# Identity transposes in TensorE's planned pauses, and low-rank products in row groups of their own, in a twelve-stage decoder on one core

## The chip, the core and the metric

The kernel runs on one core of one Trainium2 chip. The metric is the device time of one execution in microseconds (us), as the median of several runs. The core's engines, each with its own instruction stream, are TensorE (PE, matrix products; its weight loads appear as PEld), VectorE (DVE), ScalarE (ACT), GpSimd (POOL) and SyncE (SP, which here issues most DMAs). TensorE's clock can be throttled; the profile reports the granted clock as a share of full speed.

## The reference

The reference is a pre-norm decoder of four layers on x of shape 4 x 256 x 128 in f32, with a context of 4 x 512 x 96. Every layer has self-attention, cross-attention and a feed-forward part, each added to the residual:

```python
x = x + _L0_attn_ref(_layernorm(x, axis=-1), L0_attn_W, L0_attn_b)
x = x + _L0_xattn_ref(_layernorm(x, axis=-1), ctx_768, ...)   # 16 heads of 64, low-rank terms, 4 image tokens
x = x + _L0_ffn_ref(_layernorm(x, axis=-1), ...)              # grouped attention and 8 experts
...
x = x + _L3_attn_ref(_layernorm(x, axis=-1), ...)
x = x + _L3_xattn_ref(_layernorm(x, axis=-1), ctx_768, ...)
x = x + _L3_ffn_ref(_layernorm(x, axis=-1), ...)              # itself 6 layers of local attention and gated feed-forward
```

What the change touches in the arithmetic's layout is the first cross-attention. There each of the four weights has a low-rank term of rank 32:

```python
def _lora(t, down, up, alpha):
    return t @ down @ up * (LORA_W * alpha[0] / RANK)
q_in = x @ Wq + _lora(x, q_down, q_up, q_alpha)
k_in = org_ctx @ Wk + _lora(org_ctx, k_down, k_up, k_alpha)
v_in = org_ctx @ Wv + _lora(org_ctx, v_down, v_up, v_alpha)
out = _attention(q_in, k_in, v_in) + _attention(q_in, ipa_ctx @ Wk_ipa, ipa_ctx @ Wv_ipa)
return out @ Wo + bo + _lora(out, o_down, o_up, o_alpha)
```

## The kernel before

All four batches stay in SBUF as x (two tiles of 128 tokens by 128 features each). The twelve stages are written out as small named operations, per batch and per pair of heads: attn0, X0, F0, A1, X1, ffn1, A2, xattn2, ffn2, attn3, X3 (class `Net`), then six layers of local attention (class `LocalBlock`, from about 1130 us on). The string `ORDER` (L2496) interleaves the stages' batches as they are written: "attn0 X0 attn0 X0 attn0 F0 ...", so batch 0 of the first attention comes ahead of the first cross-attention's weights.

No operation is issued where it is written. `Flow.op` (L188 on) records it with its engine, a cost in us and a lateness from the table `NET` (L2236) or `LOCAL`, its reads and writes, and the buffers that it needs. `Flow.order` (L208) then plays a list schedule: it keeps a time for each engine, takes the engine whose next operation can start first, and among the operations that can start then, the one with the smallest due time. The due time is the running sum of TensorE's costs up to the operation's unit, less the rest of its own chain, plus its lateness. A buffer of a kind with a few slots (the eight PSUM banks among them) is given out when its last users have ended in this play. `Flow.issue` (L309) emits the operations in the order found; on the chip every engine runs its own list strictly in that order and waits on semaphores for true dependences. So the plan's times fix only the order; the chip's times are its own. A pause of TensorE in the plan is the time between the end of its last operation there and the planned start of the next.

Ahead of the plan, `Decoder.prepare` (L85) makes the identity on GpSimd, issues the loads of x, of columns, rows and the context, and builds masks.

The change and the prediction's steps touch these places:

- `Net.mm` (L393) and `Net.transpose` (L396): every product and every transpose of `Net`; a transpose is one product with the 128 x 128 identity as the moving operand.
- `Net.fetch` (L403, DMA issue at L410): one weight load on SP's queue into one buffer.
- `one_head` (attn0): n_turn (two transposes), h_qk, h_v, h_scores, h_max (L534), h_exp (L541), h_turn (four transposes), h_pT (copy), h_weigh (four products), h_add (L565).
- `low_rank` (L803): for each of q, k, v and o a fetch of the 32 x 1024 factor (kind x4, four slots) and of the small factor (kind e2, five slots), a scaling of the small one by alpha / 32 on DVE (l_scale, L813), then for each half of 512 columns a product (l_mm, planned at 0.9 us on TensorE) into one bank and an addition to the weight on DVE (l_add, L833). All factors lie in partitions 0 to 31. The products of o are four small ones per half.
- `image_keys` (L836): two sets of eight products with the 16 image-token columns (i_kv), after which `cross_wide` (L616) begins: p_v, p_k, p_q, p_scores and so on.
- L1796: every product of the local block; L2012 and L2086 its transposes (turn, turn_p), L2002 and L2045 the GpSimd products ahead of them.

Of the kernel before, what the change touches and what calls it, by code (L numbers as in the profile page):

```python
# [26 lines left out]
ALU = mybir.AluOpType  # L27
# [3 lines left out]
P = 128  # L31
B, S, D = 4, 256, 128
NCTX, CD = 512, 96
# [5 lines left out]
RANK = 32  # L39
# [103 lines left out]
class Flow:  # L143
# [17 lines left out]
    REST = 2.5  # L161
    STALL = 1.0
    WAIT = 5.0

    def __init__(self, parts, slots, lags, tables, tiles, free, dense, port, after):
        self.kinds = {name: (*kind, *part[1:]) for part in parts for name, kind in part[0].items()}
# [41 lines left out]
    def order(self):  # L208
        bases = self.bases()
        left = dict.fromkeys(sorted(bases), 0)  # L210
        for op in reversed(self.ops):
            op["tail"] = op["w"] + max(
                [op["lag"] + o["tail"] for o in op["next"] if o["unit"] == op["unit"]], default=0.0
            )
            op["from"] = bases[op["unit"]] - op["tail"]
            op["due"] = op["from"] + op["late"]
            op["open"] = len({id(o) for o in op["needs"]})
            op["ready"] = 0.0
            left[op["unit"]] += 1
        free = dict.fromkeys(self.LAG, 0.0)  # L220
        self.made = made = dict.fromkeys(self.slots, 0)
        self.held = {k: [None] * n for k, n in self.slots.items()}
        table, shape, rest, port, done, oldest = None, "whole", -9.0, 0.0, [], 0
        units = list(left)
        waiting = {e: [op for op in self.ops if op["eng"] == e and not op["open"]] for e in free}

        def when(op):

            at, takes, new = op["ready"], [], {}
            for b in [b for b in {id(b): b for b in op["bufs"]}.values() if b.kind is not None and b.slot is None]:  # L230
                n = new[b.kind] = new.get(b.kind, -1) + 1
                if b.kind not in self.free and b.turn != n + made[b.kind]:
                    return None
                if n == 0:
                    new[b.kind, "free"] = self.vacant(b.kind)
                if n >= len(new[b.kind, "free"]):
                    return None
                since, slot = new[b.kind, "free"][n]
                at = max(at, since)
                takes.append((b, slot))  # L240
            return at, takes

        while len(done) < len(self.ops):
            best = None
            while not left[units[oldest]]:
                oldest += 1
            limit = bases[units[oldest]] + self.AHEAD
            for e, ops in waiting.items():
                times = [
                    (max(free[e], can[0], port * op["port"]), op, can[1])  # L250
                    for op in ops if op["from"] < limit and (can := when(op)) is not None
                ]
                if times:
                    first = min(t for t, *_ in times)
                    late = lambda o: o["due"] + (
                        (o["patience"] if o["tiles"][0] != shape else 0.0)
                        + (self.WAIT if o["dense"] and first < rest + self.REST else 0.0) if e == "PE" else 0.0
                    )
                    pick = min((c for c in times if c[0] <= first + 1e-6), key=lambda c: (late(c[1]), c[1]["i"]))
                    if best is None or first < best[0]:  # L260
                        best = first, *pick[1:]
            assert best, "no operation can start"
            at, op, takes = best
            e = op["eng"]
            op["at"] = at
            if op["table"] and op["table"] != table:
                at, table = at + self.TABLE, op["table"]
            if e == "PE":
                at += self.SWITCH * (op["tiles"][0] != shape) + self.STALL * (op["dense"] and at < rest + self.REST)
                shape = op["tiles"][1]  # L270
            op["end"] = free[e] = at + op["w"]
            if op["dense"]:
                rest = op["end"]
            if op["port"]:
                port = op["end"]
            waiting[e].remove(op)
            left[op["unit"]] -= 1
            for b, slot in takes:
                b.slot = slot
                made[b.kind] += 1  # L280
                self.held[b.kind][slot] = b
            for o in {id(o): o for o in op["next"]}.values():
                o["open"] -= 1
                o["ready"] = max(o["ready"], op["end"] + op["lag"])
                if not o["open"]:
                    waiting[o["eng"]].append(o)
            done.append(op)
        return done

    def vacant(self, kind):  # L290

# [17 lines left out]
    def issue(self):  # L309
        for op in self.order():  # L310
            for b in op["bufs"]:
                if b.kind is not None and b.t is None:
                    b.t = b.make(b.slot)
            op["fn"]()


# [14 lines left out]
class Net:  # L331
# [21 lines left out]
    def __init__(self, ctx, d):  # L353
# [4 lines left out]
        at, most = _layout(LocalBlock.LAYOUT, LocalBlock.TILES)  # L358
# [8 lines left out]
            {k: "e" for k in NET if k.endswith("_exp")} | {"exp": "e", "gelu": "g"}, NET_TILES | LOCAL_TILES,  # L367
            ("bank", *LocalBlock.TILES), ("scores", "weigh"), PORT, after,
        )
        self.n = 0  # L370
        self.x = [Buffer() for _ in range(B)]

# [30 lines left out]
    def fetch(self, kind, *parts):  # L403

        w = self.buf(kind)

        def dma():
            for name, lo, hi, rows, view in parts:
                out = w.t[:rows, lo:hi]
                self.nc.sync.dma_start(out=out if view is None else view(out), in_=self.a[name])  # L410

        self.op("fetch", dma, [], [w])
        return w
# [389 lines left out]
    def low_rank(self, w):  # L803

        nc, d = self.nc, self.d
        for m, rows in (("q", D), ("k", CD), ("v", CD), ("o", RANK)):
            low, high = ("down", "up") if m != "o" else ("up", "down")
            n = rows if m != "o" else D
            big = self.fetch("x4", (f"x0_{m}{high}", 0, 1024, RANK, None))
            small = self.fetch("e2", (f"x0_{m}{low}", 0, n, RANK, None))  # L810

            def scale(m=m, small=small, n=n):
                nc.vector.tensor_scalar(  # L813
                    small.t[:RANK, :n], small.t[:RANK, :n], d.col(f"x0_{m}al", rows=RANK), 1.0 / RANK,
                    ALU.mult, ALU.mult,
                )

            self.op("l_scale", scale, [small], [small])
            for h in range(2):
                ps = self.buf("bank")  # L820
                cut = slice(h * 512, (h + 1) * 512)

                def product(m=m, rows=rows, big=big, small=small, ps=ps, cut=cut, h=h):
                    if m != "o":
                        self.mm(ps.t[:rows, :], small.t[:RANK, :rows], big.t[:RANK, cut])
                        return
                    for i in range(4):
                        g = 4 * h + i
                        self.mm(ps.t[:, i * D : (i + 1) * D], big.t[:RANK, g * P : (g + 1) * P], small.t[:RANK, :D])

                r = rows if m != "o" else P
                self.op("l_mm", product, [big, small], [ps])
                self.op("l_add", lambda m=m, r=r, cut=cut, ps=ps: nc.vector.tensor_add(  # L833
                    w[m].t[:r, cut], w[m].t[:r, cut], ps.t[:r, :]), [ps, w[m]], [w[m]])

    def image_keys(self):  # L836

# [860 lines left out]
    def write(self):  # L1698
        stages = {name: getattr(self, f"stage_{name}")() for name in STEPS if name != "F3"}
        self.last = LocalBlock(self)  # L1700
# [4 lines left out]
        self.last.write()  # L1705

    def stage_attn0(self):
        w = self.fetch("ws", ("a0_w", 0, 384, P, None))
        for b in range(B):
            self.one_head(b, w, P, 1.0 / math.sqrt(128.0), True, False)  # L1710
            yield
# [519 lines left out]
def slots():  # L2231
# [9 lines left out]
    "n_scale": ("DVE", 0.55, -8.91),  # L2241
    "n_scale4": ("DVE", 1.18, 121.06),
    "n_turn": ("PE", 0.25, 0.35),
    "n_out": ("ACT", 0.34, 8.73),
    "add": ("DVE", 0.45, 11.52),
    "fetch": ("SP", 0.3, -134.71),
# [250 lines left out]
attn0 X0 attn0 X0 attn0 F0 X0 F0 attn0 F0 X0 A1 F0 F0 A1 X1 F0 F0 A1 X1 F0 ffn1 A1 X1 ffn1 A2 X1 A2  # L2497
ffn1 xattn2 A2 ffn1 xattn2 ffn2 A2 xattn2 attn3 ffn2 X3 xattn2 attn3 ffn2 X3 attn3 ffn2 X3 in attn3 in X3 in in
"""
STEPS = ("attn0", "X0", "F0", "A1", "X1", "ffn1", "A2", "xattn2", "ffn2", "attn3", "X3", "F3")  # L2500


# [171 lines left out]
```

## Time and profile before

| | |
|---|---|
| median of 3 runs | 2126.19 us (2120.12 to 2128.97) |
| the profiled execution, its own time | 2128.02 us |
| its span, first to last instruction | 2126.2 us |
| mean granted clock of TensorE | 0.977 |
| PE busy | 2036.1 us, 24181 instructions |
| PE weight loads busy | 1346.7 us |
| DVE, ACT, POOL busy | 1638.7, 1178.9, 990.8 us |
| transposes at L396 | 257.1 us, 1757 instructions |
| chain that ended last | PE 69%, DVE 21%, POOL 5%, issue 3%, ACT 2%, DMA 1% |

How to read it: the page first gives busy time by engine over the whole span, then the span in 40 slices of 53 us with the busy share in tenths, TensorE's granted clock in the row PEclk and DMA traffic. Groups of instructions follow by source line; a line such as L393 is a helper that all stages share, so groups are told apart by their shapes ("64*128 64x512" is a stationary operand of 64 rows by 128 columns and a moving one of 64 rows by 512 columns). The list of waits says for which instruction's result an engine stood still. In the timeline each row is a start, a duration, the engine, the operation and how many instructions were merged; in brackets stands the idle time before it and what ended it. Windows give, for a stretch, its length, each engine's busy time and instruction count, then the granted clock, the DMA share and GB/s. An f32 product appears as two records, a transpose as one.

### The profile page before, as it was taken

The numbers are of one execution on the slowest core, as the hardware profiler recorded it, in microseconds if no ns is written. First come the engines' busy times: TensorE is split into PE (matmuls) and PEld (weight loads), VectorE is DVE, ScalarE is ACT, GpSimd is POOL, SyncE is SP. The second block draws the span as 40 slices with busy tenths as digits, with TensorE's granted clock in tenths as the row PEclk, the third lists the DMA queues.
The fourth block names the chain that finished last, engine by engine and source line by source line (L and its number), as shares of the span: only waits on it lengthen the run. The fifth ranks groups of instructions, "written<-read, shape, count | busy, mean of one in ns | idle before, by whom it ended". The sixth has DMA issues, their size and how long they took to land.

```text
span 2126.2 us, 59285 instructions
## 1 busy us (share of the span) xinstructions
PE 2036.1 (96%) x24181; PEld 1346.7 (63%) x24181; DVE 1638.7 (77%) x4352; ACT 1178.9 (55%) x2668; POOL 990.8 (47%) x1155
## 2 busy tenths in 40 slices
PE   7999999999999999799999998999999999999997
PEld 4566585767665666566665656666656666666665
DVE  3766777788778678988887688789788787897882
ACT  1754736444545686476565564555556556556553
POOL 2333424331312234455365357557567465575660
PEclk6999999999999999899999999999999999999998
DMA  5000020011020000100000102112121121211101
GB/s 154 1 1 1 1 66 6 31 31 58 9 76 2 9 2 2 35 27 1 1 1 1 51 14 69 42 26 79 42 72 49 28 69 43 71 46 42 29 22 31
DMA packets 33422, 71.16 MB, mean 33 GB/s; under 512 B 5688, under 2 KB 17984, under 8 KB 33152
## 3 DMA queue, kind: packets, MB, share of 16 engines
q1 hardware_dynamic: 20320, 50.29, 8.0%
q10 hardware_dynamic: 12832, 17.09, 2.5%
q8 instruction: 191, 3.13, 0.6%
q14 instruction: 79, 0.65, 0.1%
HBM read 41.68 MB, written 0.52 MB: 20 GB/s over the span
## 4 chain that ended last, share of the span: by engine, by line
PE 69%; DVE 21%; POOL 5%; issue 3%; ACT 2%; DMA 1%; POOLq 0%; SPq 0%; ACTq 0%; DVEq 0%
PE bank L393 39%; PE bank L1796 18%; PE bank L396 9%; PE bank L2012 2%; DVE arena L1950 2%; DVE arena L1960 2%; POOL arena L2002 2%; DVE arena L1965 2%; POOL arena L1964 1%; DVE arena L1573 1%; POOL arena L2045 1%; PE bank L2086 1%; DVE arena L2053 1%; DVE arena L2055 1%; DVE arena L1985 1%
## 5 line engine op out<-in xcount | busy, mean ns | idle before, releaser
L393 PE MATMUL bank<-arena 128*64 128x256 f32 (+11 forms) x6824 | 875.6, 395 | 11.5 <-ACT arena L1495 3.6
L393 PEld LDWEIGHTS bank<-arena 128*128 128x128 f32 (+4 forms) x6824 | 540.1, 166 | 291.1 <-issue 108.1
L1796 PE MATMUL bank<-arena 64*64 64x32 f32 (+3 forms) x13584 | 653.9, 251 | 11.4 <-ACT arena L2109 4.8
L1796 PEld LDWEIGHTS bank<-arena 64*64 64x64 f32 (+2 forms) x13584 | 387.9, 127 | 217.9 <-issue 119.8
L401 ACT COPY arena<-bank 128x512 f32<-128x512 f32 (+4 forms) x586 | 270.0, 489 | 295.2 <-PE bank L393 209.2
L396 PE MATMUL bank<-ident,arena 128*128 128x128 f32 x1757 | 257.1, 282 | 36.1 <-DVE arena L440 16.9
L396 PEld LDWEIGHTS bank<-ident,arena 128*128 128x128 f32 x1757 | 199.0, 143 | 134.3 <-issue 46.0
L1964 POOL TENSOR_TENSOR arena<-arena 128x1024 f32<-128x1024 f32 x96 | 226.5, 2363 | 123.1 <-DVE arena L1950 63.0
L675 POOL TENSOR_SCALAR arena<-arena 128x508 f32<-128x508 f32 (+1 forms) x256 | 175.8, 693 | 209.2 <-DVE arena L672 183.9
L670 ACT ACTIVATE arena<-bank,arena 128x508 f32<-128x508 f32 (+1 forms) x256 | 175.3, 691 | 79.1 <-DVE arena L668 36.6
L2002 POOL TENSOR_TENSOR arena<-arena 128x1024 f32<-128x1024 f32 x96 | 180.8, 1903 | 71.9 <-DVE arena L1986 71.9
L1958 ACT ACTIVATE arena<-bank 128x512 f32<-128x512 f32 x192 | 114.0, 601 | 133.3 <-PE bank L1796 106.3
L668 DVE TENSOR_REDUCE arena<-bank 128x1 f32<-128x508 f32 (+1 forms) x256 | 164.3, 678 | 17.9 <-PE bank L393 17.7
L972 ACT ACTIVATE arena<-bank 128x512 f32<-128x512 f32 (+1 forms) x256 | 124.5, 582 | 64.1 <-PE bank L393 62.7
L401 DVE COPY arena<-bank 128x512 f32<-128x512 f32 (+1 forms) x196 | 125.9, 668 | 43.5 <-PE bank L396 29.6
L1960 DVE TENSOR_TENSOR arena<-bank,arena 128x512 f32<-128x512 f32 x192 | 127.7, 684 | 39.9 <-ACT arena L1958 38.7
L2045 POOL TENSOR_TENSOR arena<-arena 128x1024 f32<-128x1024 f32 x48 | 91.4, 1903 | 108.5 <-ACT arena L2018 62.7
L1950 DVE TENSOR_TENSOR arena<-bank,arena 128x256 f32<-128x256 f32 x384 | 138.8, 413 | 3.1 <-ACT arena L1958 2.7
L949 DVE TENSOR_REDUCE arena<-bank 128x1 f32<-128x512 f32 (+2 forms) x256 | 116.9, 515 | 21.4 <-PE bank L393 21.0
L2018 ACT COPY arena<-bank 128x512 f32<-128x512 f32 x192 | 103.1, 601 | 28.8 <-PE bank L2012 28.8
L1965 DVE TENSOR_REDUCE arena<-arena 128x16 f32<-128x1024 f32 x96 | 114.4, 1204 | 0.0
L430 POOL TENSOR_TENSOR arena<-arena,neghalf 128x2 f32<-128x2 f32 (+1 forms) x56 | 41.3, 742 | 156.4 <-DVE arena L429 139.2
(227 smaller groups left out, 2424.2 us busy)
## 6 DMA issues: line engine op xcount, KB each, us to landing
arena<-arena SPq DMA_DIRECT2D x48, 384.0 KB, 4.0
arena<-in_f_w SPq DMA_DIRECT2D x24, 512.0 KB, 3.5
arena<-in_f_wqkv ACTq DMA_DIRECT2D x18, 512.0 KB, 6.8
arena<-arena SPq DMA_DIRECT2D x48, 128.0 KB, 2.3
arena<-in_f_wo ACTq DMA_DIRECT2D x6, 512.0 KB, 3.6
arena<-in_f_w ACTq DMA_DIRECT2D x6, 341.0 KB, 3.9
arena<-in_f_w ACTq DMA_DIRECT2D x6, 192.0 KB, 6.6
arena<-in_x_wq SPq DMA_DIRECT2D x2, 512.0 KB
```

What stands on the lines that cost most here:

```text
L393: self.nc.tensor.matmul(out, lhsT, rhs, start=start, stop=stop)
L396: self.nc.tensor.transpose(out, in_, self.d.ident)
L401: return self.op(name, lambda: copy(out(), in_()), reads, writes, holds)
L668: self.op("p_max", lambda ps=ps, one=one: nc.vector.tensor_reduce(one(nmx), ps.t[:, :n], AX.X, ALU.max, negate=True), [ps], [most], [nmx])
L670: self.op("p_exp", lambda ps=ps, one=one, cols=cols: nc.scalar.activation(cols(), ps.t[:, :n], AF.Exp, bias=one(nmx), accum_out=one(sums)) ...
L675: nc.gpsimd.tensor_scalar(cols(), cols(), one(sums), 1.0, ALU.mult, ALU.mult)
L1796: self.nc.tensor.matmul(out, lhsT, rhs, start=start, stop=stop)
L1950: nc.vector.tensor_mul(heads(tmp.t[:, cut])[:, :, lo : lo + 32], heads(ps.t)[:, :, 32 - lo : 64 - lo], spread(1, lo, lo + 32),)
L1960: op("cosine", lambda cut=cut, ps=ps: nc.vector.tensor_mul(heads(out.t[:, cut]), heads(ps.t), spread(0, 0, 64)), [ps, w["tab"]], [out])
L1964: op("rotary", lambda: nc.gpsimd.tensor_add(out.t, out.t, tmp.t), [out, tmp], [out])
L1965: op("norms", lambda: nc.vector.tensor_reduce(ss.t[:, at : at + 16], heads(sq.t), AX.X, ALU.add), [sq], [ss])
L2002: nc.gpsimd.tensor_mul(heads(out.t), heads(out.t), rs.t[:, at : at + 16, None].to_broadcast([P, 16, 64]))
```

## The change

It has three parts.

1. `low_rank`: the factors of q, k, v and o are loaded into partitions 0-31, 32-63, 64-95 and 96-127. One l_mm operation per half of the columns issues the products of q, k and v one after the other, into three banks taken together; it reads the factors of all three. The six l_adds follow. The two operations of o come after these, reading partitions 96 to 127. In the plan the six l_mm of q, k and v become two, each at the same cost of 0.9 us.
2. A new operation warm, planned first: 34 transposes of the identity into a bank, written at the head of the first stage.
3. `Flow.order` notes, for each TensorE operation that takes new banks and starts more than 9 us into the plan after a planned pause of over 0.7 us, a number of fillers: 0.7 of the time for which TensorE and the bank are both free, divided by 0.11 us. `Flow.issue` emits that many transposes of the identity into the operation's own bank directly ahead of it. The played times do not contain the fillers.

```diff
+    IDLE = 0.7
+    FILL = 0.11
+    SETTLED = 9.0
...
             op["at"] = at
+
+            op["fill"] = [
+                (b, int(0.7 * (at - max(free[e], self.since(b.kind, slot))) / self.FILL))
+                for b, slot in takes if b.kind == "bank" and at - free[e] > self.IDLE
+            ] if e == "PE" and at > self.SETTLED else []
...
+    def since(self, kind, slot):
+        b = self.held[kind][slot]
+        return max((o["end"] + o["lag"] for o in b.users), default=0.0) if b is not None else 0.0
...
+            b, n = max(op["fill"], key=lambda f: f[1], default=(None, 0))
+            for _ in range(n):
+                self.keep(b)
             op["fn"]()
...
+        self.flow.keep = lambda b: self.transpose(b.t[:, :P], d.ident)
...
-                out = w.t[:rows, lo:hi]
+                out = w.t[rows if isinstance(rows, slice) else slice(rows), lo:hi]
...
     def low_rank(self, w):
...
-        for m, rows in (("q", D), ("k", CD), ("v", CD), ("o", RANK)):
+        parts = {}
+        for i, (m, rows) in enumerate((("q", D), ("k", CD), ("v", CD), ("o", RANK))):
+
+            r = slice(RANK * i, RANK * (i + 1))
...
+            big = self.fetch("x4", (f"x0_{m}{high}", 0, 1024, r, None))
+            small = self.fetch("e2", (f"x0_{m}{low}", 0, n, r, None))
...
+            parts[m] = big, small, r, rows
+        for h in range(2):
+            cut = slice(h * 512, (h + 1) * 512)
+            made = {m: self.buf("bank") for m in "qkv"}
+
+            def products(made=made, cut=cut):
+                for m, ps in made.items():
+                    big, small, r, rows = parts[m]
+                    self.mm(ps.t[:rows, :], small.t[r, :rows], big.t[r, cut])
+
+            self.op("l_mm", products, [b for m in "qkv" for b in parts[m][:2]], list(made.values()))
...
     def stage_attn0(self):
+        warm = self.buf("bank")
+        self.op("warm", lambda: [self.transpose(warm.t[:, :P], self.d.ident) for _ in range(WARM)], [], [warm])
...
+    "warm": ("PE", 0.1, -300.0),
...
+WARM = 34
```

More of the change, by code (lines that the diff above doesn't have):

```diff
@@ L805, in low_rank, with scale @@
         nc, d = self.nc, self.d
-        for m, rows in (("q", D), ("k", CD), ("v", CD), ("o", RANK)):
+        parts = {}
+        for i, (m, rows) in enumerate((("q", D), ("k", CD), ("v", CD), ("o", RANK))):
+            r = slice(RANK * i, RANK * (i + 1))
             low, high = ("down", "up") if m != "o" else ("up", "down")
             n = rows if m != "o" else D
-            big = self.fetch("x4", (f"x0_{m}{high}", 0, 1024, RANK, None))
-            small = self.fetch("e2", (f"x0_{m}{low}", 0, n, RANK, None))
-            def scale(m=m, small=small, n=n):
+            big = self.fetch("x4", (f"x0_{m}{high}", 0, 1024, r, None))
+            small = self.fetch("e2", (f"x0_{m}{low}", 0, n, r, None))
+            def scale(m=m, small=small, n=n, r=r):
@@ L813, in scale @@
                 nc.vector.tensor_scalar(
-                    small.t[:RANK, :n], small.t[:RANK, :n], d.col(f"x0_{m}al", rows=RANK), 1.0 / RANK,
-                    ALU.mult, ALU.mult,
+                    small.t[r, :n], small.t[r, :n], d.col(f"x0_{m}al")[r], 1.0 / RANK, ALU.mult, ALU.mult,
                 )
             self.op("l_scale", scale, [small], [small])
[L819 to L834, printed above, removed]
@@ new lines, in low_rank @@
+            parts[m] = big, small, r, rows
[7 more added lines that the diff above has]
+            self.op("l_mm", products, [b for m in "qkv" for b in parts[m][:2]], list(made.values()))
+            for m, ps in made.items():
+                n = parts[m][3]
+                self.op("l_add", lambda m=m, n=n, cut=cut, ps=ps: nc.vector.tensor_add(
+                    w[m].t[:n, cut], w[m].t[:n, cut], ps.t[:n, :]), [ps, w[m]], [w[m]])
@@ new lines, in low_rank, with product @@
+        big, small, r, _ = parts["o"]
+        for h in range(2):
+            ps = self.buf("bank")
+            cut = slice(h * 512, (h + 1) * 512)
+            def product(ps=ps, h=h):
+                for i in range(4):
+                    g = 4 * h + i
+                    self.mm(ps.t[:, i * D : (i + 1) * D], big.t[r, g * P : (g + 1) * P], small.t[r, :D])
+            self.op("l_mm", product, [big, small], [ps])
+            self.op("l_add", lambda cut=cut, ps=ps: nc.vector.tensor_add(
+                w["o"].t[:, cut], w["o"].t[:, cut], ps.t), [ps, w["o"]], [w["o"]])
```

## The prediction

> **What bounds the kernel now.** I read the page's head first, then TensorE's waits, then its order of time at the start, then granted clocks in 1 us slices.
>
> ```profile
> span 2126.2 us, 59285 instructions
> ...
> PE   7999999999999999799999998999999999999997
> ...
> DVE  3766777788778678988887688789788787897882
> ...
> PEclk6999999999999999899999999999999999999998
> ```
>
> TensorE (PE) is busy in nearly every slice, VectorE (DVE) in about eight tenths. PEclk is below 9 in the first slice (53 us), around 800 us and at the end. A PE-bound kernel gains from less PE work, from a higher PE clock and from shorter pauses. So: where are the pauses?
>
> ```profile
> PE bank L396 <- DVE arena L440: 16.9, 6, 10.0
> PE bank L2012 <- POOL arena L2002: 12.8, 15, 1.4
> PE bank L2086 <- POOL arena L2045: 9.4, 7, 3.2
> PE bank L396 <- POOL arena L1578: 5.7, 2, 4.5
> ```
>
> Columns: total us, times, longest. 10.0 is the wait for the first layernorm. Going through PE's timeline I count 44 pauses of 0.7 us or more, 71.7 us together: 10.0 at the start, 3.6 in the rest of the first 53 us, 0.7 between 53 and 800 (one pause), 14.2 from 800 to 1000, 11.1 from 1000 to 1300, 32.1 (29 pauses) after. From 53 to 780 PE is busy for 722.4 of 727 us (99.4%), its parts added up.
>
> The start in order of time (start, us, what), PE alone:
>
> ```profile
> 11.65 4.45 PE L393 MATMUL bank<-arena 128*128 128x256 f32 x12 [0.46 <-ACT arena L401]
> 17.47 0.90 PE L396 MATMUL bank<-ident,arena 128*128 128x128 f32 x4 [1.38 <-ACT arena L541]
> 20.60 12.61 PE L393 MATMUL bank<-arena 32*128 32x512 f32 x20 [2.23 <-DVE arena L813]
> 33.00 1.90 PE L393 MATMUL bank<-ctxT,arena 96*128 96x508 f32 x2
> 34.83 3.78 PE L393 MATMUL bank<-arena 32*128 32x128 f32 x16
> 40.40 6.85 PE L393 MATMUL bank<-ctxT,arena 96*128 96x16 f32 x32
> 57.82 1.04 PE L396 MATMUL bank<-ident,arena 128*128 128x128 f32 x8
> ```
>
> An f32 product shows as two records. The x20 group is the six low-rank products of q, k, v (12 records) and the first h_weigh (8, from 31.1): 10.5 us for six products, 1.75 each. A transpose costs 0.225 us here (0.90/4) and 0.13 later (1.04/8). The gap is the clock:
>
> ```profile
> 21.00:22.00 1.00, 1.00 (x2) 0.37 (x2) 0.00 (x0) 0.00 (x0) 0.00 (x0) 0.50 0.00 0
> ...
> 52.00:53.00 1.00, 1.00 (x5) 0.56 (x6) 0.00 (x0) 0.59 (x1) 0.00 (x0) 0.59 0.00 0
> 53.00:54.00 1.00, 1.00 (x8) 0.28 (x4) 0.47 (x3) 0.00 (x0) 0.00 (x0) 1.00 0.00 0
> ```
>
> The third number from the end is the granted clock: 0.50 until 52.8 us though PE has been busy without a hole since 20.6. Before 18.7 the rows print 1.00, but the x12 group (1,152 columns in two records each, 4.45 us; at 54.28 us eight records of 512 columns take 3.70, by which these would need 2.1) and the 0.225 us transposes show half speed already. Twelve us of products on 32 rows did not raise the clock; it rose after 5.7 us of products on 96 and 128 rows.
>
> **Part 1, the low-rank products.** The six products of q, k, v now lie in rows 0-31, 32-63, 64-95 and run as two groups of three. That three such products overlap, no row shows; the nearest has two 64-row products of 512 columns:
>
> ```profile
> 807.05 1.02 PE L393 MATMUL bank<-arena 64*128 64x512 f32 x4
> ```
>
> Two products took 1.02 us, where one alone needs 0.85 (1.75 halved, less latency). So a group of three costs between 1.75 us (full overlap) and 5.25 (none) at half clock; I take 1.85, the near row's overlap. Two groups: 3.7 instead of 10.5, so 6.8 us less. Each waits for what was queued for it:
>
> ```profile
> 12.90 7.34 DMA arena<-in_x_qdown
> 20.24 0.03 issue
> 20.27 0.29 DVE arena L813
> ```
>
> The first product waited for the small factor's DMA (landed 20.24) and one scale. Now it waits for the factors of k and v also; those were issued up to 0.9 us later, yet three scales ran back to back in 0.63 us from 20.27, so all had landed: 0.4 us later, with h_weigh and p_k queued behind on PE. The eight fetches stay eight of the same size on SP's queue; o's pair no longer stands behind products. The six l_adds (0.685 us each) can no longer hide between products: from 22.9 they run to 27.0, k's last to 26.4, when h_weigh ends too (24.7 plus 1.7). p_k then starts near 26.6, not 33.0: 6.4 us less, all on the path, since PE has one pause from there to 800. Eight banks exist and three are taken at once; no other product asks for them then.
>
> **Part 2, the clock of the start.** Warm-up: 34 transposes by 0.225 us are 7.7 us, from about 1.6 (identity made) to 9.3; the first true transpose starts at 10.01. They cost nothing; if each took 0.27 us (median of the rows), they would end at 10.8, and PE still idles 1.4 and 2.2 us before 20.6. They do not carry to 20.6 by themselves: PE then has nothing between about 16.6 and 21. What counts is after 21: two groups on 96 rows, h_weigh on 128, p_k on 96, some 7 us without a thin product, as long as what raised the clock at 52.8. So the clock is up near 27, not 52.8. Of 19.6 us of PE work from 33.0 to 52.6, 8.3 are long products (halved: 4.2) and 11.3 are loads of weights and transposes (0.21-0.225 to 0.13-0.14: about 3.8). Together 8 us; bounds 0 and 10, I take 7, as thin products may lower the clock for a while.
>
> **Part 3, fillers in the planned pauses.** The number is not in the trace: for each pause that the planner expects over 0.7 us, 0.7 of it divided by 0.11. If the plan's pauses are those of the trace after the first (43, 61.7 us), 393 transposes, 51 us at 0.13: inside the pauses, 0.83 of each. Cost: from 0 (each inside a true pause) to 51 and more (none is). I take 3.5, 27 fillers outside, because the planner's costs are near the rows (rotary 2.38, row 2.36; p_turn 0.47, row 0.52), so its pauses should be. A filler writes the bank of the operation behind it, so it waits for nothing that this operation didn't.
>
> Gain: after longer pauses the clock is 0.50 again: nine stretches from 811 to 2114 hold 48 us of PE work. By part 2's ratio (8 of 19.6) 20 us at most; half of it lies where DVE is as busy as PE (0.9 and more around 855-880 and 1299-1307), so 10 on the path; the fillers reach most: 8.
>
> A rule speaks against this. The Trainium skill, "TensorE: Matmul & The Clock Gate", Part 4, says that full clock does not engage for transposes, which don't count as busy. The rows:
>
> ```profile
> 1684.48 1.97 PE L2012 MATMUL bank<-ident,arena 128*128 128x128 f32 x8 [1.40 <-POOL arena L2002]
> 1686.24 3.96 PE L1796 MATMUL bank<-arena 128*128 128x512 f32 x12
> ```
>
> The clock is 0.50 from 1684.4 and 1.00 from 1687.2: 1.8 us of transposes and 1.0 of products raised it. Elsewhere (853.6 to 861.6) 1.5 us of products and more than twice as much transposing did. So I let transposes count; by the rule the 8 us fall away. The same page's window of 3.4 idle us before the clock falls is not what 1684.4 shows: 1.4 us sufficed after small products.
>
> **Sum.** 6.4 + 7 + 8 - 3.5 = 18 us less. The profiled execution took 2128.0 (span 2126.2 and 1.8 around it), so 2110; that is 1.8 above the median of the runs, so on the median 2108.
>
> **Rivals.**
> Fillers where there is no pause (0.22): one mechanism, PE's strict order. The plan has pauses that the chip fills, above all in 53 to 800, where the trace has one; there each filler costs its 0.13 us. Break-even: 18/0.13, some 140 more fillers outside pauses. If the plan pauses twice as long as the trace, 785 fillers, 102 us against 61.7: 40 lost, 21 gained: 2145. For it: PE is at 99.4% from 53 to 780. Against: the costs fit the rows.
> The gate ignores transposes (0.20), as the skill has it: 6.4 + 7 - 3.5, 10 less: 2116. Against: 1684 and 858.
> The planner moves (0.12): l_mm is charged 3.6 us instead of 7.2, so every later due time shifts alike, but its play of events shifts unevenly and picks another order, which the tuned due times do not fit. I give it 0.5% of loss, eating most: 2124. The trace can't tell.
>
> **How the numbers follow.** Forecast 0.46: 2108, own range 2095 to 2115. Below 0.5% (2115.6 to 2136.8 is no change that a measurement here can tell) I put nearly all of the forecast and a part of the second and third rival: faster 0.52; same 0.25; slower 0.23, nearly the first rival. The range reaches from the forecast's low end to most of the first rival: 2095 to 2140.
>
> **What would show it.** Right: two groups of three products near 21, p_k near 26.6, clock 1.00 by 28, PE's first true transpose still near 10, few slices under 1.00 after 800, pauses filled. Wrong: identity transposes between 53 and 800 with the stages there longer; clock still 0.50 after 30, or falling in filled pauses; the same work in another order with new waits.

## The result, and the profile after

| | before | after |
|---|---|---|
| median | 2127.3 us (14 runs, 2119.8 to 2134.1) | 2117.7 us (14 runs, 2111.1 to 2120.4) |
| ratio | | 0.9956 (95% interval 0.9943 to 0.9969): 9.4 us less |
| profiled execution: span, mean granted clock | 2126.2 us, 0.977 | 2118.5 us, 0.986 |

The direction was forecast, the size was not: about half of the 18 us came. The head of the page of after:

```profile
span 2118.5 us, 59911 instructions
...
PE   8999999999999998899999999999999999999998
...
PEclk8999999999999999999999999999999999999999
```

The clock's dip in the first slice is smaller, and those near 800 us and at the end no longer show in slices of 53 us (804 to 808 is still at half clock). 317 more TensorE records ran: the program holds 318 identity transposes, 34 for the warm-up, 45 before 27 us and 239 later. With these left out, TensorE's 24,181 records come in the same order in both profiles but for 18 of the first 92 (one record is missing from the trace of after): behind the start the planner did not pick another order. TensorE's waits (total us, times, longest), for the four rows shown of before:

```profile
PE bank L2044 <- POOL arena L2034: 12.2, 15, 1.4
PE bank L2118 <- POOL arena L2077: 9.2, 7, 2.1
PE bank L412 <- DVE arena L456: 8.5, 4, 4.4
```

The first two are almost unchanged (12.8 and 9.4 before): between 1290 and 2077 us, where the local block's transposes wait, the plan put no filler. In the third the wait of 10.0 us for the first layernorm is now 2.5, the rest being warm-up; the 4.4 near 1120 us is still open. The fourth (5.7 us before, for L1578) is no longer among the long ones.

The start of after, TensorE alone:

```profile
1.59 5.92 PE L412 MATMUL bank<-ident 128*128 128x128 f32 x34 [1.59 <-POOL ident masks.py:199]
...
15.49 2.69 PE L412 MATMUL bank<-ident 128*128 128x128 f32 x21
18.02 0.60 PE L412 MATMUL bank<-ident,arena 128*128 128x128 f32 x4
20.03 3.65 PE L409 MATMUL bank<-arena 32*128 32x512 f32 x20 [1.42 <-DVE arena L832]
23.51 2.78 PE L412 MATMUL bank<-ident 128*128 128x128 f32 x24
27.15 2.05 PE L409 MATMUL bank<-arena 32*128 32x128 f32 x16 [0.85 <-DVE arena L832]
29.12 8.48 PE L409 MATMUL bank<-ctxT,arena 96*128 96x16 f32 x34
```

The same 20 records that took 12.61 us take 3.65. But the next is not p_k, as I had it: it is o's low-rank products (32*128 32x128), ahead of which 24 fillers stand and TensorE still waits 0.85 us for L832, the scaling of o's factor. Then the image products (96x16, 32 of the 34 records) and the product behind them run 8.48 us, from 29.6 on at half clock:

```profile
28.00:29.00 1.00, 1.00 (x11) 1.00 (x9) 1.00 (x4) 0.00 (x0) 0.64 (x2) 1.00 1.02 414
29.00:30.00 1.00, 1.00 (x8) 0.88 (x8) 1.00 (x3) 0.00 (x0) 0.19 (x1) 0.81 0.90 356
30.00:31.00 1.00, 1.00 (x6) 1.00 (x6) 0.72 (x2) 0.00 (x0) 0.00 (x0) 0.50 0.68 188
```

TensorE is busy in all three rows (1.00 after the length), and the clock (third from the end) falls from 1.00 to 0.50, to come back at 39.9 us.

DVE's 4,352 instructions come in the same order in both programs, but for 22 places before 48 us. So each can be matched with itself, and the difference of its starts tells where time was won or lost. In the two profiles the lead is 10.4 us at 58 us, level to 540, 7.8 at 784, 10.7 at 890, 6.8 at 1136, 5.5 at 2104 and 7.6 at the end. I call this the lead below. It is read from one execution each: after, start_only, no_mid and seen (below) are one program up to 440 us, and their leads at 58 us are 10.4, 9.5, 8.7 and 8.9.

### The profile page after: what moved, and what is told of

The parts are those of the page before. It is cut to its first block, busy times and chain, and to the rows that moved or that the text cites. A ratio compares the mean times of both kernels' runs of the same rounds, so it can differ in the third digit from the quotient of the medians.

```text
span 2118.5 us, 59911 instructions
## 1 busy us (share of the span) xinstructions
PE 2050.2 (97%) x24498; PEld 1373.6 (65%) x24499; DVE 1638.8 (77%) x4352; ACT 1179.3 (56%) x2668; POOL 993.1 (47%) x1155
## 4 chain that ended last, share of the span: by engine, by line
PE 68%; DVE 22%; POOL 5%; issue 3%; ACT 2%; DMA 1%; POOLq 0%; SPq 0%; ACTq 0%; DVEq 0%
PE bank L409 39%; PE bank L1828 17%; PE bank L412 9%; PE bank L2044 2%; DVE arena L1982 2%; DVE arena L1992 2%; DVE arena L1997 2%; POOL arena L2034 2%; DVE arena L1603 1%; POOL arena L1996 1%; POOL arena L2077 1%; PE bank L2118 1%; DVE arena L2085 1%; DVE arena L417 1%; DVE arena L2087 1%
## 5 line engine op out<-in xcount | busy, mean ns | idle before, releaser
L409 PE MATMUL bank<-arena 128*64 128x256 f32 (+11 forms) x6824 | 857.5, 393 | 10.5 <-ACT arena L1525 3.6
L409 PEld LDWEIGHTS bank<-arena 128*128 128x128 f32 (+4 forms) x6824 | 532.6, 165 | 276.8 <-issue 100.0
L412 PEld LDWEIGHTS bank<-ident,arena 128*128 128x128 f32 x1757 | 196.6, 141 | 116.2 <-issue 47.3
L2044 PEld LDWEIGHTS bank<-ident,arena 128*128 128x128 f32 x768 | 87.0, 142 | 42.0 <-POOL arena L2034 21.8
```

The lines of the kernel that those rows point to most:

```text
L409: self.nc.tensor.matmul(out, lhsT, rhs, start=start, stop=stop)
L412: self.nc.tensor.transpose(out, in_, self.d.ident)
```

## The experiments

Ratios are to the kernel before, timed on the same chip, with 95% intervals; us are worked out on 2127.3.

**No filler after the start (start_only).**

```diff
-            ] if e == "PE" and at > self.SETTLED else []
+            ] if e == "PE" and 100.0 > at > self.SETTLED else []
```

> The changed kernel without its 239 fillers after the first 30 us (the 34 of the warm-up and the two groups of 21 and 24 stay). Theory A (the gain is made in the first 53 us, the later fillers cost what they bring): 10 us under before, ratio 0.9945 to 0.9955, and the same within 3 us as the changed kernel; in the profile the lead of 10.4 us at the first p_scores stays level from 440 to 784 us. Theory B (the later fillers bring the 8 us forecast less 3.5, and chance in the clock's windows hid it): 4 to 5 us slower than the changed kernel, ratio about 0.998.

Ratio 0.9972 (0.9962 to 0.9983), 6.0 us less. Lead 9.5 at 58 us, and level from 440 to 784 (9.5 at both). The profile is as theory A has it; the time lies between the theories: the later fillers together bring something like 3 us (about 0 to 7, so not clear of noise).

**No filler, warm-up and row groups kept (no_fill), and row groups alone (rows_only).**

```diff
-    SETTLED = 9.0
+    SETTLED = 1e9
...
-WARM = 34
+WARM = 0
```

The second hunk is in rows_only alone.

> The changed kernel with warm-up and row groups, but no filler at all. Theory A says the row groups are worth 6.4 us and the clock between 20 and 53 us the other 4: without fillers at 15 and 23 us TensorE is at half clock from 20, the two groups of products take 3.7 us instead of 1.8, and the clock rises near 27 to 30: 6 to 9 us under before (ratio 0.996 to 0.997). Rival (the fillers at 15 and 23 are idle work, the row groups do it all): 10 us under before, as the changed kernel.

> The row groups alone: no warm-up, no filler. The warm-up ends at 7.5 us and nothing carries its clock to 20: both theories expect the same as with the warm-up and without fillers, within 1 us, 6 to 9 us under before. If the warm-up's quicker first head (h_scores ends earlier) reached the path, this one would be slower by up to 2 us.

Ratios 1.0000 (0.9992 to 1.0008) and 0.9994 (0.9983 to 1.0004): no gain that the measurement can tell, where I had expected 6 to 9 us. The lead at 58 us is 3.9 and 4.4. A miss, and the profile of rows_only shows why. DVE and TensorE in order of time:

```profile
27.63 0.61 DVE L581 SCALAR_TENSOR_TENSOR x<-bank,arena,x 128x128 f32<-128x128 f32 x2 [2.43 <-issue]
28.16 0.68 DVE L850 TENSOR_TENSOR arena<-arena,bank 128x512 f32<-128x512 f32 x1
28.75 0.29 DVE L440 BATCH_NORM_STATS2 arena<-x 128x6 f32<-128x128 f32 x1
...
30.67 0.29 DVE L832 TENSOR_SCALAR arena<-arena,cols 32x128 f32<-32x128 f32 x1
30.99 0.68 DVE L850 TENSOR_TENSOR arena<-arena,bank 96x512 f32<-96x512 f32 x1
31.05 1.19 PE L409 MATMUL bank<-arena 32*128 32x128 f32 x4 [3.52 <-issue]
```

The scaling of o's factor (L832) stands on DVE's list behind h_add (L581, which waits for h_weigh), an l_add and the next batches' statistics (L440 on). Its data had been fetched some ten us earlier. TensorE, whose list has o's products next, stands for 3.52 us. In the kernel before that wait lay behind other products. The low-rank products and h_weigh before it, in no_fill:

```profile
21.70 6.33 PE L409 MATMUL bank<-arena 32*128 32x512 f32 x20 [3.56 <-DVE arena L832]
```

**Warm-up and fillers, products as before (no_rows).** The kernel after with the low_rank of before; the plan then has no group of 24 fillers near 23 us.

> Warm-up and all fillers, but the low-rank products as before, one after the other on 32 rows. Theory A: the row groups' 6.4 us are lost, the clock part stays only if 32-row products keep the clock up, which the profile of before speaks against: 0 to 3 us under before, ratio 0.9985 to 1.0005. Rival (the warm clock is what matters, the six products then take 5.3 us instead of 10.5): 5 to 8 us under before, ratio 0.9965 to 0.9975.

Ratio 0.9992 (0.9982 to 1.0003), 1.7 us less; as theory A. TensorE at the products:

```profile
21.14 11.57 PE L409 MATMUL bank<-arena 32*128 32x512 f32 x20 [2.56 <-DVE arena L829]
```

The clock is at 0.50 from 22.2 to 53.0 us, after fillers as without them. In no_mid and seen, with row groups, it fell near 22 us too, after waits of 2.4 and 2.2 us, but was back at 29. So in the time of the whole kernel neither part alone shows a gain; at 58 us this version leads by 0.2 us and the row groups without fillers by about 4, against 8.7 to 10.4 for both together. The reading is that the fillers need products on more rows behind them, and the row groups need something for the new wait.

**The image products made wider (wide_kv).**

```diff
-                        ps.t[:, 4 * B * g : 4 * B * (g + 1)], wi.t[:CD, g * P : (g + 1) * P],
-                        d.ctxT[:, :, NCTX - IPA :],
+                        ps.t[:, 16 * B * g : 16 * B * (g + 1)], wi.t[:CD, g * P : (g + 1) * P],
+                        d.ctxT[:, :, NCTX - 16 :],
...
```

> The changed kernel, with the 16 image-token products on 64 columns (the last 16 of each batch) instead of 16, the wanted columns picked in the copy after them; output as before. Theory A (the clock falls at 29 us because thin products count for little, though TensorE is busy): the clock stays 1.00 from 29 to 39, the products take about 5 us instead of 8.2, 3 to 5 us less than the changed kernel, ratio to before about 0.994. Rival (it falls because of a window in which TensorE waited for o's factor): clock 0.50 again from 29 to 39, no gain or a loss of up to 1 us.

Ratio 0.9957 (0.9939 to 0.9974), as after. The clock fell all the same, from 31 to 41 us, and the same 34 records took 7.4 us instead of 8.48. Theory A falls: 64 moving columns are no better than 16. The rival isn't shown either; see the open points.

**o's scaling moved up, the fillers ahead of o's products left out (scale_moved).**

```diff
-        for op in self.order():
+        done, groups = self.order(), 0
+        o_scale = [op for op in done if op["name"] == "l_scale"][3]
+        done.remove(o_scale)
+        done.insert(next(i for i, op in enumerate(done) if op["name"] == "h_add"), o_scale)
+        for op in done:
...
+            groups += n > 0
+            if n > 0 and groups == 2:
+                n = 0
```

> The changed kernel with the scaling of o's small factor moved ahead of h_add on DVE, and without the 24 fillers that stand ahead of o's products. Theory A (a new wait took the place of the one removed: o's products now follow at once and stand behind DVE's statistics of the next batch): o's products start near 23.6 instead of 27.2 us, 3 us less than the changed kernel, ratio about 0.994. Rival (something else, the image weights' DMA, is just as late): the image products start at 26 or later and under 1.5 us is gained.

Ratio 0.9960 (0.9945 to 0.9975): no gain. The wait is gone (o's products follow h_weigh without a gap), but in its profile the factors' DMA let the first group start at 21.6 instead of 20.0, after 3.0 us without work, and the clock was 0.50 from 22 to 42. That start is set by the landing of q's small factor and lies between 19.7 and 22.9 us in the 14 profiles, so one profile can't tell why the median didn't gain. That the wait and the clock have to be mended together was the guess that best (below) tests.

**Row groups alone, with the scaling moved (rows_scale).** The two edits of rows_only, and the first five added lines above.

> The row groups alone (no warm-up, no filler) with the scaling of o's small factor moved ahead of h_add. Theory A (the forecast's 6.4 us were there, and DVE's order took 3.5 of them back): the lead at 58 us is 7 to 8 us instead of 4.4, ratio to before 0.9965 to 0.998. Rival (the image weights' DMA is next and as late): the lead stays at 4 to 5 us, ratio 0.999.

Ratio 0.9975 (0.9964 to 0.9986), 5.3 us less; lead 7.6 at 58 us. As theory A: without a filler and without warm-up, moving one DVE instruction turned 1.3 us into 5.3 (a difference of about 1 to 7). Behind h_weigh TensorE goes on at 27.4 us, in rows_only at 31.05.

```profile
21.19 10.02 PE L413 MATMUL bank<-arena 32*128 32x512 f32 x36 [2.61 <-DVE arena L836]
```

The 36 records are both groups, h_weigh and o's products in one piece.

**No filler between 440 and 790 us (no_mid).**

```diff
...
+            groups += n > 0
+            if n > 0 and 3 <= groups <= 15:
+                n = 0
```

> The changed kernel without the 94 fillers between 440 and 790 us (13 places). Theory A (there the plan pauses and the chip does not): the lead of 10.4 us stays level to 784 instead of falling to 7.8, 2 to 3 us less than the changed kernel, ratio about 0.9945. Rival (the fillers lie in pauses too short to see, and the fall by 2.6 has another cause): no difference, 0.9956.

Ratio 0.9934 (0.9917 to 0.9952), 4.7 us less than after by the ratios (interval of the difference about 0 to 9). Against after, it gains 2.6 us between 540 and 763 us in the profile, as expected. Two of the rows taken out, as they are in after:

```profile
615.71 1.69 PE L412 MATMUL bank<-ident 128*128 128x128 f32 x14
...
634.75 1.16 PE L412 MATMUL bank<-ident 128*128 128x128 f32 x9
```

94 such transposes, some 12 us at 0.13, stand where before had no pause of 0.7 us or more. Against start_only, no_mid differs by the 145 fillers after 800 us: 0.9972 to 0.9934, 8 us gained (about 4 to 12).

**Twice the fillers (double).** FILL 0.055 instead of 0.11.

> The changed kernel with twice the fillers everywhere (614 instead of 318, the 34 of the warm-up unchanged), in the same places. Theory A prices a filler outside a pause at 0.13 us: 296 more are 38 us, of which the pauses that are still open there (about 10 us from 800 to 900 and at the end) hide a part: 20 to 30 us slower than the changed kernel, ratio to before 1.005 to 1.010. Rival (the fillers are hidden, since TensorE has slack that the profile counts as busy): under 10 us slower.

Ratio 1.0016 (1.0002 to 1.0030), 12.8 us over after for 296 more: 0.04 us for each, a third of what a transpose takes, at a mean clock of 0.992 in the profile. That lies between the theories: less than I had priced, more than the rival's 10. Between 548 and 763 us the lag on after grows by 7.2 us for some 90 more, 0.08 each; elsewhere they may lie in pauses or pay in clock, which was not taken apart.

**Fillers where the profile has the pauses (seen), and with the start mended (best).** seen is no_mid with this table, looked up by an operation's name and its number among those of that name; best adds ("l_mm", 0): 12, moves o's scaling, and drops the 24 fillers ahead of o's products.

```diff
+SEEN = {("turn", k): 9 for k in (32, 64, 96, 128, 160)} | {("turn", k): 5 for k in (72, 104, 136)}
+SEEN |= {("turn_p", 0): 12, ("turn_p", 6): 9, ("turn_p", 22): 7, ("turn_p", 38): 7, ("turn_p", 54): 7, ("turn_p", 70): 9}
+SEEN |= {("n_turn", 45): 28, ("n_turn", 51): 7, ("c_turn", 48): 7}
...
+            k = op["name"], kinds.get(op["name"], 0)
+            kinds[op["name"]] = k[1] + 1
+            if k in SEEN:
+                b, n = b or next(b for b in op["bufs"] if b.kind == "bank"), n + SEEN[k]
```

> The changed kernel without the 94 fillers between 440 and 790 us, and with 153 more, put by hand ahead of the 17 operations that paused 0.9 us or more for a result (not for a bank) in its profile: seven to nine ahead of the local block's transposes, 28 ahead of the layernorm transpose near 1120, 12 near 1292. Theory A (what pays is a filler in a pause that the chip has; nothing is lost there): no cold stretch at 1118, 1292, 1678, 1818, 1958, and 4 to 8 us under the kernel with the 94 left out, ratio to before 0.990 to 0.992. Rival (pauses and cold windows change place from run to run, so that fillers put where one profile shows a pause don't find it): same as that kernel, 0.9934.

> The one before, with the scaling of o's small factor moved ahead of h_add, the 24 fillers ahead of o's products left out, and 12 more ahead of the first low-rank products. Theory A (the clock then stays up from 15 us over the wait for the factors' DMA, and o's products follow at once): p_scores first at 38 to 39 us instead of 42, 3 us under the kernel before, ratio 0.988 to 0.991. Rival (the clock falls all the same after the products on 32 rows, and the wait for the DMA takes up what is saved): no difference to the kernel before.

seen: 0.9913 (0.9899 to 0.9928), as theory A; against no_mid (0.9934) the 4 us are not clear of noise, but TensorE's pauses of 0.7 us or more fell from 48.2 to 25.6 us in all. The half-clock stretches that after has near 1118, 1678, 1818 and 1958 are gone; that at 1291 is not, and a new one lies at 640 to 647, where its order is that of no_mid, which has none there. best: 0.9894 (0.9876 to 0.9913), median 2102.3 us against 2126.0: it beats the kernels before and after; its 4 us on seen are, by the ratios, not clear of noise. Its clock row and its start:

```profile
PEclk9999999999999999999999999999999999999999
```

```profile
15.54 2.46 PE L428 MATMUL bank<-ident 128*128 128x128 f32 x21
17.83 0.60 PE L428 MATMUL bank<-ident,arena 128*128 128x128 f32 x4
18.27 1.47 PE L428 MATMUL bank<-ident 128*128 128x128 f32 x12
19.73 5.62 PE L425 MATMUL bank<-arena 32*128 32x512 f32 x36
25.28 6.17 PE L425 MATMUL bank<-ctxT,arena 96*128 96x16 f32 x34
```

No pause from 15.5 to 31 us; the image products begin at 25.3 instead of 29.1, the first p_scores at 36.5 instead of 41.9, and the lead at 58 us is 15.9, which is 7.0 more than in seen.

**The kernel before once more (before_again).**

> The kernel before, unchanged, for a second profile. If chance places the windows of half clock (theory: the same program, the same order, but a clock gate whose windows run free of it), its cold stretches lie elsewhere than in the first profile: some of those at 810, 854, 1128, 1684, 1739 are gone, others appear (near 1025 and 1120, where every changed version has one), and from 820 to 1136 us it is 1 to 2 us longer than the first profile. Rival (the changed versions lose there for a reason of their own): the same stretches as the first profile, within 0.5 us.

0.9996 (0.9983 to 1.0009). The theory falls: after 800 us the stretches of half clock are the first profile's, at 812, 853, 870, 1126, 1296, 1682, 1737, 2082 and 2102, and from 820 to 1136 this execution was only 0.2 us longer than the first. At the start it does differ: the clock was up from 37 to 40 us, and it led the first profile by 1.5 us at 58.

## Why the size was wrong

**The step that failed** is "p_k then starts near 26.6, not 33.0: 6.4 us less, all on the path", and the 7 us of clock put on top of it. The start was to give 13.4 us; it gave 6.0 (3.6 to 8.1, start_only). Another wait, for o's scaling, took the place of the one removed, and the clock did not stay up.

- The products themselves: right in kind. In no_fill both groups and h_weigh took 6.33 us at half clock. h_weigh's eight records, 0.21 us apart, are some 1.7 of them, so a group is (6.33 - 1.7)/2 = 2.3 us, not 1.85; at full clock it is (3.65 - 0.9)/2 = 1.4.
- What is late next: missed. I wrote that o's pair "no longer stands behind products" and took p_k for the next in line. o's products are next, and DVE's list holds their scaling behind h_add and four statistics: a wait of 3.5 us took the place of the one removed. rows_only against rows_scale shows it: 1.3 us against 5.3, by that one move, which comes near the 6.4 forecast. I had followed the l_adds on DVE's list and not this l_scale.
- The clock: I had it up near 27 us and staying. In after it was up from 16 to 29.6, kept there by fillers at 15 and 23 that the forecast hadn't placed (in no_fill it fell at 19), and then fell for 10.2 us in the image products, which the forecast allowed 1 of its 8 us for.
- The yardstick: the profile before may have had a slow start. before_again led it by 1.5 us at 58 us, so the leads there may be 1 to 2 us too large.
- Two readings of the clock. The transposes at 17.47 us do not show half speed: the clock was up from 15.3 to 18.7, and each took 0.27 to 0.33 us from start to end, as at full clock in after (0.42 to 0.48 at half). The 0.90 us of the four hold a wait: the third started 0.29 us after the second. That 0.225 is close to the 0.213 between starts in the warm-up at half clock is luck. And near 1684 the clock was back at 1687.8, not 1687.2, so 1.6 us of products stood beside the 1.8 of transposes.

**The later fillers' gain** (8 us) was right in size: 145 fillers after 800 us brought about 8 (4 to 12), their own cost taken off. Part of that is luck, for they did not reach "most" pauses: of the 61.7 us after the first, some 44 are left. In the profiles no_mid draws ahead of start_only by 1.8 us from 784 to 1136 us, 5.6 to 2075 and 8.7 to the end; after 2075 us the mean clock of after is 0.96 instead of 0.82.

**Their cost** (3.5 us for 27 outside a pause): right in size by luck, 4.7 by the ratios and 2.6 in the profile, for it came from 94 fillers between 440 and 790 at about 0.05 us, not from 27 at 0.13. The first rival named the mechanism, the region and why, but the fillers there were 94 of 318 and not the most of 785. Its break-even was too low: double's 296 more cost 12.8 us and not 38.

The three parts, 6.0, 8 and -4.7, add up to the 9.4 measured because each is a difference of two of the same ratios; the sum is no check of its own. The second rival, that the gate ignores transposes, is refuted by the warm-up (below); the third, another order of the plan, by TensorE's records, which come in the same order behind the start.

**Open.** After, start_only, no_fill, rows_only, no_rows, scale_moved and rows_scale each have a half-clock stretch between 1020 and 1035 us and one of 6.8 instead of 3.4 us near 1120; neither profile of the kernel before has them, though the order of TensorE's work is the same there. But wide_kv and no_mid, whose program there is that of after, lack the first, and their second lasts 3.4 us; so the program alone does not place them. In the two profiles wide_kv keeps a lead of 11.3 us from 1000 to 1136 where after falls from 9.2 to 6.8. What places them is open. Nor is it settled why the clock falls in the image products: 64 columns instead of 16 don't prevent it (wide_kv), the wait ahead of o's products isn't needed for it (best, 28.3 to 35.1), and the products on 32 rows before them were not tried apart.

## What to carry to other kernels

Where a stall is removed, walk every engine's list behind it, not only the bottleneck's: an instruction of 0.3 us that the planner put behind unrelated work was the next limit here. Filler work pays in pauses that a profile shows and costs where only a plan has them; here moving a part of the fillers from the one to the other, with the new wait mended, made 22 us out of 9. Two parts that each yield little may yield together, so an ablation that only takes one part away tells less than it seems.

## What the runs showed of the hardware

Transposes alone raise TensorE's clock. In the warm-up of after nothing else runs, and the count of transposes that each us touches (the number behind the first busy time) goes from 7 and 6 to 11, for their starts are 0.213 us apart up to 5.5 us and 0.109 from 5.8 on:

```profile
2.00:3.00 1.00, 1.00 (x7) 1.00 (x6) 0.00 (x0) 0.00 (x0) 1.00 (x5) 1.00 0.89 247
...
4.00:5.00 1.00, 1.00 (x6) 1.00 (x6) 0.93 (x5) 0.00 (x0) 1.00 (x5) 1.00 0.82 204
...
6.00:7.00 1.00, 1.00 (x11) 1.00 (x10) 1.00 (x2) 0.00 (x0) 1.00 (x3) 1.00 1.08 225
```

The clock column says 1.00 in all of them: before its first recorded change, here that to 1.00 at 5.7 us, it can't be relied on, and the durations must be read instead. So the rule that the prediction quotes against itself does not hold for these transposes.

The busy share of the profile does not tell the clock: products on 32 rows kept TensorE busy for 10 us and more at 0.50 in before and in no_rows, and in best it fell at 28.3 us under image products, though TensorE had had no pause since 15.5. In each of the 14 profiles all recorded changes lie on one grid of 3.413 us, whose place against the program varies (in before_again it lies 1.2 us later than in before). After the first 60 us the stretches of half clock lasted 3.4, 6.8 or 10.2 us, those cut off by the end apart. So the pause of 1.4 us at 1684 was followed by 3.4 us at half speed. From run to run of the changed kernel the time goes with the clock: 2118 to 2120 us at a mean of 0.986, 2111 to 2115 at 0.990 and 0.991.
